# Making gate and up of a ternary feed-forward beside the self-attention, and sharing the program's end between two engines

## The chip, the cores and the metric

The kernel runs on one core of a Trainium2 chip. The metric is the device time of one execution in microseconds, as the median of three runs. The core has five engines that run their own instruction queues: TensorE for matmuls (PE in the profile, with its weight loads shown as PEld), VectorE (DVE), ScalarE (ACT), GpSimd (POOL) and SyncE (SP), which here only issues transfers. Each engine takes its queue in the order in which the program was compiled.

## The reference

A decoder of two layers, batch 4, sequence 512, width 512, float32. There are six phases, each followed by a residual addition and a layer norm over the width:

```python
x = layernorm(x + L0_attn(x))          # phase A: one head of 512, rotary positions
x = layernorm(x + L0_xattn(x, ctx))    # phase B: 8 heads over channels, against a context
x = layernorm(x + L0_ffn(x))           # phase C: ternary weights
x = layernorm(x + L1_attn(x))          # phase D: 16 heads
x = layernorm(x + L1_xattn(x, ctx))    # phase E
x = layernorm(x + L1_ffn(x))           # phase F: fp4 weights, then y / rms(y)
```

Two parts bear on the change. The first feed-forward uses weights of three values, made in the kernel from float32 weights:

```python
def weight_quant(w):
    scale = 1.0 / clip(mean(abs(w)), 1e-5)
    return clip(round(w * scale), -1.0, 1.0) / scale

gate = act_quant(x) @ weight_quant(w_gate).T      # w_gate, w_up: 2048 x 512
up   = act_quant(x) @ weight_quant(w_up).T
out  = act_quant(fwht(silu(gate) * up)) @ weight_quant(w_down).T
```

And the very end of the program is, for the last batch, `y / sqrt(mean(y*y) + 1e-6)`, added to x, and the layer norm of the sum, `(x - m) / sqrt(v + 1e-5)`.

## The kernel before

The work is written as generators. Phases A to F exist for each of the four batches (A0 to A3, B0 and so on). `lanes` keeps two such tasks alive, takes a step of each in turn, and starts the next when a task says so. After every step `step` also advances background generators, each beside a fixed stretch of tasks: C0 beside A1 to A3, the weights of phase C ("C") beside B0 to B2, others later. A class `Pipe` delays a piece of work by a number of steps (`later(n, fn)`, run down by `tick`; `drain` runs it empty, a step at a time).

What comes out is a list of instructions for each engine. A scheduler fixes their order at compile time from costs and due times, and `tc.issue_after(x)` keeps an instruction behind x in its own engine's order. Transfers are nearly all issued by SP, in turn; a transfer whose buffer isn't free, or whose data aren't made yet, holds those behind it. Buffers come from pools: "o" with 69 of 2 KB per partition, "w" with four (for raw weights, `tw`), "t" with 13, "x" with 12, and 8 banks of PSUM.

Phase A, for a batch (`l0_attn`): eight products qk of 12 matmuls each (every float32 product is made of a high and a low part, hence three matmuls for one); ACT adds the bias (L340); DVE and POOL turn by the rotary angles (L349 on DVE, L352 on POOL) and POOL joins the halves (L357), after which ACT and POOL split the result into high and low. The values are made next, then four score products `as`, softmax (L398 on DVE, L400 on ACT), the transposed scores as `ap`, cast by ACT to `aph`, and the products `pv` with the values. POOL also adds a bias to x (L408), DVE adds the product and takes statistics (L425, L211), and the norm's root and four norms follow (L217 to L238). The transposed low part of the next x is made by POOL (L146, tile `xTl`).

Phase B, for a batch, has 16 iterations of one shape: six matmuls of scores `bs` (L526), the maximum on DVE (L474), the exponential on ACT (L476), the sum and reciprocal on DVE (L480), a scaling on POOL (L482), eight transposes (L248), copies of these out of PSUM on DVE or ACT (L489) and four products `bo` (L498).

The ternary weights come in 48 chunks of 128x512, 16 for each of gate, up and down (`wg_t`, `wu_t`, `wd_t`). `l0_ffn_scales` (C0) reads all 48 beside A and sums their absolute values on DVE (L558); for each matrix one matmul with ones (L569) adds over partitions, and L571 and L572 make mean and scale. `l0_ffn_weights` ("C") reads all 48 again beside B. DVE multiplies by the scale and adds a large constant, MAGIC, which rounds (L587), and clips to MAGIC-1 to MAGIC+1 (L588); ACT subtracts MAGIC and writes bf16 (L596), two chunks into one tile `tb` of 2 KB, which stays in SBUF for phase C.

The end (`l1_ffn`, last batch): ACT squares the four accumulators with a running sum (L1214), DVE takes the mean (L1217) and the inverse root by a seed and three Newton steps (`rsqrt`, L166 to L176); then for each of four row tiles the scaled addition (L1220) and the statistics (L211, L212); `finish` makes the second root on DVE and the four norms (L235) and stores (L238).

Of the kernel before, what the change touches and what calls it, by code (L numbers as in the profile page):

```python
# [10 lines left out]
F32 = mybir.dt.float32  # L11
F32R = mybir.dt.float32r
F16 = mybir.dt.float16
BF16 = mybir.dt.bfloat16
# [8 lines left out]
P = 128  # L23
NT = 4
# [44 lines left out]
class Net:  # L69
    def __init__(self, ctx, tc, args):  # L70
# [22 lines left out]
        self.gu_codes = scratch("gu_codes", (22, P, 512))  # L93
        self.xd = [args["x"]] + [scratch(f"x{i}", (B, S, D)) for i in range(1, 6)] + [args["out"]]
# [235 lines left out]
    def l0_attn(self, b):  # L330
# [7 lines left out]
        def evac(ps, w, m):  # L338
            z = zs[w, m] = self.t("z")
            nc.scalar.activation(z, ps, AF.Identity, bias=self.qkb[:, w * NT + m : w * NT + m + 1], scale=1.0 if w else P ** -0.5)  # L340
            if m % 2:
                pipe.later(1, turn, w, zs[w, m - 1], z)
# [200 lines left out]
    def l0_ffn_scales(self):  # L543

        nc = self.nc
        self.had = self.c("had", [P, P], F32R)
        self.had16 = self.load(self.c("had16", [P, P]), self.a["had16"])
        f = self.t("had")
        nc.gpsimd.dma_start(f[:, 0:P], self.a["had"])
        pipe = Pipe()  # L550
        pipe.later(3, nc.vector.tensor_copy, self.had, f[:, 0:P])
        for name in self.TERNARY:
            chunks = self.ternary_chunks(name)
            part = self.c(name + "_abs", [P, len(chunks)])

            def absum(f, n):
                with self.tc.issue_after(self.mark.ins):
                    nc.vector.tensor_reduce(part[:, n : n + 1], f, AX.X, ALU.add, apply_absolute_value=True)  # L558

            for n, (k, c, ap) in enumerate(chunks):  # L560
                pipe.tick()
                pipe.later(1, absum, self.load(self.w("tw"), ap), n)
                yield
            yield from pipe.drain()
            m = self.c(name + "_mean", [P, 4])
            nc.vector.tensor_reduce(m[:, 2:3], part, AX.X, ALU.add)
            yield
            ps = self.pb("tot")
            nc.tensor.matmul(ps[:, 0:1], self.ones, m[:, 2:3], start=True, stop=True)  # L569
            yield  # L570
            nc.vector.tensor_scalar(m[:, 0:1], ps[:, 0:1], 1.0 / (len(chunks) * P * 512), 1e-5, ALU.mult, ALU.max)  # L571
            nc.vector.reciprocal(m[:, 1:2], m[:, 0:1])  # L572
            self.mean[name], self.scale[name] = m[:, 0:1], m[:, 1:2]

    def l0_ffn_weights(self):

        nc = self.nc
        yield from self.bg["C0"]
        pipe = Pipe()
        order = [("wg_t", x) for x in self.ternary_chunks("wg_t")]  # L580
        up = [("wu_t", x) for x in self.ternary_chunks("wu_t")]
        order = [e for c in range(4) for e in order[4 * c : 4 * c + 4] + up[4 * c : 4 * c + 4]]
        order += [("wd_t", x) for x in self.ternary_chunks("wd_t")]
        cur = []

        def quant(name, k, c, f):
            nc.vector.tensor_scalar(f, f, self.scale[name], MAGIC, ALU.mult, ALU.add)  # L587
            nc.vector.tensor_scalar(f, f, MAGIC + 1.0, MAGIC - 1.0, ALU.min, ALU.max)  # L588
            pipe.later(1, put, name, k, c, f)

        def put(name, k, c, f):
            if not cur:
                cur.append(self.o("tb", BF16, 1024))
            o = cur[0][:, 0:512] if len(cur) == 1 else cur[0][:, 512:1024]
            cur.append(o)
            nc.scalar.activation(o, f, AF.Copy, bias=-MAGIC)  # L596
            self.tern[name][k, c] = o
            if len(cur) == 3:
                cur.clear()

        for name, (k, c, ap) in order:
            pipe.tick()
            pipe.later(1, quant, name, k, c, self.load(self.w("tw"), ap))
            yield
        yield from pipe.drain()
# [510 lines left out]
    def l1_ffn(self, b):  # L1116
# [31 lines left out]
        def gate(o):  # L1148
            nc.scalar.activation(o, o, AF.Silu)
            y["gate"] = o  # L1150
# [43 lines left out]
        if b + 1 < B:  # L1194
# [16 lines left out]
            return  # L1211
        for i in range(NT):
            sq = self.t("fsq")
            nc.scalar.activation(sq, acc[i], AF.Square, accum_out=ss[:, i : i + 1])  # L1214
            if i % 2:
                yield
        nc.vector.tensor_scalar(ve, ss, 1.0 / 512.0, 1e-6, ALU.mult, ALU.add)  # L1217
        r = self.rsqrt(ve, fm[:, 8:20])
        for i in range(NT):
            nc.vector.scalar_tensor_tensor(x[i], acc[i], r[:, i : i + 1], x[i], ALU.mult, ALU.add)  # L1220
            self.ln_stats(x[i], i, ln)
            if i % 2:
                yield
        self.finish(pipe, x, ln, 5, b)
        yield from pipe.drain()
# [35 lines left out]
def body(tc, args, phases=range(6)):  # L1261
    with ExitStack() as ctx:
# [4 lines left out]
        net.bg = {("B", 0): net.l0_xattn_ctx(0), "C0": net.l0_ffn_scales(), "C": net.l0_ffn_weights(), "D": net.l1_attn_weights(), "F0": net.l1_ffn_codes(), "F": net.l1_ffn_weights()}  # L1267
# [82 lines left out]
```

## Time and profile before

| | us |
| --- | --- |
| median of three runs | 1586.2 (1585.69 to 1587.84) |
| profiled execution | 1587.75 |
| its span, first to last instruction | 1586.0 |
| mean granted TensorE clock | 0.993 |

In the lists of operations, each line gives the source line, the engine, the operation and the tiles, then shapes and the count; behind the bar come the time in all, the mean of one in ns, and how long the engine sat idle before them with what ended that. Some rows of operations that the change touches or adds to, by source line:

| line | engine | what | count | ns each |
| --- | --- | --- | --- | --- |
| L587 | DVE | scale and round a chunk | 48 | 480 median |
| L588 | DVE | clip a chunk | 48 | 414 median, 384 to 1379 |
| L596 | ACT | chunk to bf16 | 48 | 626 median |
| L340 | ACT | bias to a product of phase A | 32 | 690 median |
| L408 | POOL | bias to x in phase A | 16 | 1306 median, 1289 to 1827 |
| L482 | POOL | scale an exponential in phase B | 128 | 766 mean |
| L1149 | ACT | table load, once, at 1269 us | 1 | 1283 |

In the profile's 40 slices, the busy share of each engine in tenths runs so:

```
PE   8999999999999999899999999999999999999995
DVE  6486589999976688778577697766886897889896
ACT  5333337888878877787696765968635455545552
POOL 6663663555535303430435323353234344434341
```

A slice is 39.65 us. The first six are phase A and the next five or so are phase B. The lists of transfers give a mean time from issue to landing of 3.8 us for the 32 loads of gate chunks, 3.7 for up and 2.8 for down, 256 KB each.

### The profile page before, as it was taken

Reading aid. Unit: us, or ns where it says so; the run is one execution under the profiler, and the core shown is the slowest. Engines: PE = TensorE matmul, PEld = TensorE weight load, DVE = VectorE, ACT = ScalarE, POOL = GpSimd, SP = SyncE. Lnnn points to the kernel's source line nnn. Section 1 sums busy time; section 2 is a strip of 40 time slices with the busy share of each in tenths; the row PEclk is TensorE's granted clock in tenths of the full one; section 3 lists DMA queues with packets and bytes.
Section 4 is the critical chain, followed back from the end, with each engine's and each line's share of the span. In section 5 each row is a group of like instructions: output and inputs, shape, how many; then the busy total and the mean of one; then the engine's idle time right before and its main releaser. Section 6 shows DMA issues by size and latency. Waiting matters only on the chain.

```text
span 1586.0 us, 25593 instructions
## 1 busy us (share of the span) xinstructions
PE 1515.5 (96%) x8222; PEld 1092.0 (69%) x8222; DVE 1239.8 (78%) x2676; ACT 1014.6 (64%) x2193; POOL 666.0 (42%) x672
## 2 busy tenths in 40 slices
PE   8999999999999999899999999999999999999995
PEld 6888785444544664477777768777687767787874
DVE  6486589999976688778577697766886897889896
ACT  5333337888878877787696765968635455545552
POOL 6663663555535303430435323353234344434341
PEclk9999999999999999999999999999999999999998
DMA  7053344455114644653444435543426630020101
GB/s 254 29 166 114 121 155 136 141 173 184 62 57 123 220 150 131 204 178 116 134 109 122 111 131 153 156 112 91 136 99 219 236 107 30 1 80 1 54 1 53
DMA packets 134149, 192.31 MB, mean 121 GB/s; under 512 B 17264, under 2 KB 52080, under 8 KB 134016
## 3 DMA queue, kind: packets, MB, share of 16 engines
q1 hardware_dynamic: 129888, 182.23, 36.3%
q0 software_dynamic: 4128, 8.46, 2.1%
q8 instruction: 65, 1.06, 0.3%
q14 instruction: 68, 0.56, 0.1%
HBM read 117.75 MB, written 47.71 MB: 104 GB/s over the span
## 4 chain that ended last, share of the span: by engine, by line
PE 61%; DVE 17%; ACT 8%; issue 7%; DMA 3%; POOL 3%; SPq 0%; DVEq 0%; ACTq 0%; POOLq 0%
PE fg L1185 7%; PE facc L1168 6%; PE dT L933 3%; DVE fg L1141 3%; DVE bsm L474 3%; PE pg L687 2%; PE pu L689 2%; PE dn L741 2%; ACT de L923 2%; PE had L755 2%; PE bo L498 2%; PE do L953 2%; PE qk L156 2%; PE qk L155 2%; PE qk L154 2%
## 5 line engine op out<-in xcount | busy, mean ns | idle before, releaser
L1141 DVE SCALAR_TENSOR_TENSOR fg<-fg,gs,fg 128x512 f32<-128x512 f32 x220 | 162.7, 744 | 29.1 <-ACT fg L1133 16.0
L923 ACT ACTIVATE de<-de,dm 128x128 f32<-128x128 f32 (+3 forms) x256 | 143.0, 563 | 11.4 <-DVE dm L919 11.0
L1185 PE MATMUL fg<-fxh,gu 128*128 128x512 f32 x352 | 140.4, 399 | 6.0 <-DVE fg L1141 4.3
L919 DVE CUSTOM_DVE_ANT_0 de<-ds,negm,thr 128x128 f32<-128x128 f32 (+3 forms) x256 | 126.3, 545 | 19.0 <-PE ds L908 15.8
L482 POOL TENSOR_SCALAR be<-be,bsm 128x512 f32<-128x512 f32 x128 | 96.4, 766 | 103.8 <-DVE bsm L480 68.2
L1185 PE MATMUL fg<-fxl,gu 128*128 128x512 f32 x352 | 137.3, 390 | 0.0
L664 POOL TENSOR_TENSOR hl<-g,hh 128x512 fp32r<-128x512 f32 x64 | 83.3, 1308 | 110.6 <-ACT hh L663 89.8
L1145 POOL TENSOR_TENSOR fg<-fg,fg 128x512 f32<-128x512 f32 x44 | 60.4, 1374 | 150.0 <-DVE fg L1141 54.7
L476 ACT ACTIVATE be<-bs,bsm 128x512 f32<-128x512 f32 x128 | 87.4, 690 | 31.1 <-DVE bsm L474 29.3
L845 POOL TENSOR_TENSOR dql<-dqf,dqh 128x512 fp32r<-128x512 f32 x32 | 41.4, 1294 | 150.6 <-ACT dqh L844 141.6
L933 PE MATMUL dT<-ident,de 128*128 128x128 f32 x640 | 91.3, 278 | 8.5 <-ACT de L923 6.4
L933 PEld LDWEIGHTS dT<-ident,de 128*128 128x128 f32 x640 | 71.7, 141 | 27.6 <-ACT de L923 14.8
L1185 PEld LDWEIGHTS fg<-fxh,gu 128*128 128x128 f32 x352 | 66.0, 188 | 31.2 <-DVE fg L1141 15.6
L474 DVE TENSOR_REDUCE bsm<-bs 128x1 f32<-128x512 f32 x128 | 83.3, 671 | 0.0
L498 PE MATMUL bo<-bpT,cT 128*64 128x512 f32 x256 | 77.0, 618 | 2.7 <-DVE bpT L489 1.4
L248 PEld LDWEIGHTS bT<-ident,be 128*128 128x128 f32 x512 | 54.9, 141 | 34.1 <-issue 10.4
L248 PE MATMUL bT<-ident,be 128*128 128x128 f32 x512 | 73.2, 281 | 3.7 <-POOL be L482 2.2
L1185 PEld LDWEIGHTS fg<-fxl,gu 128*128 128x128 f32 x352 | 66.1, 188 | 12.2
L352 POOL TENSOR_TENSOR z<-z,rope_cos 128x512 f32<-128x512 f32 x32 | 46.8, 1473 | 64.8 <-DVE zs L349 57.8
L1137 ACT ACTIVATE fg<-fg,gs 128x512 f32<-128x512 f32 x44 | 30.3, 689 | 67.3 <-PE fg L1185 67.2
L687 PE MATMUL pg<-qT,tb 128*128 128x512 bf16 x256 | 66.8, 381 | 4.5 <-ACT qT L649 2.8
L1133 ACT ACTIVATE fg<-fg,gs 128x512 f32<-128x512 f32 x88 | 60.1, 683 | 16.4 <-PE fg L1185 16.3
(342 smaller groups left out, 4673.2 us busy)
## 6 DMA issues: line engine op xcount, KB each, us to landing
x<-x SPq DMA_DIRECT2D x176, 256.0 KB, 3.0
had_scratch<-hw SPq DMA_DIRECT2D x64, 256.0 KB, 2.3
z<-had_scratch SPq DMA_DIRECT2D x64, 256.0 KB, 6.0
stk<-dqh SPq DMA_DIRECT2D x192, 64.0 KB, 2.1
tw<-in_wg_t SPq DMA_DIRECT2D x32, 256.0 KB, 3.8
tw<-in_wu_t SPq DMA_DIRECT2D x32, 256.0 KB, 3.7
tw<-in_wd_t SPq DMA_DIRECT2D x32, 256.0 KB, 2.8
p<-in_gu_p SPq DMA_DIRECT2D x22, 256.0 KB, 3.1
```

The lines of the kernel that those rows point to most:

```text
L248: self.nc.tensor.transpose(pt[:, i * P : (i + 1) * P], srcs[i][:, j * P : (j + 1) * P], self.ident)
L474: nc.vector.tensor_reduce(sm[:, h : h + 1], ps, AX.X, ALU.max, negate=True)
L476: nc.scalar.activation(e, ps, AF.Exp, bias=sm[:, h : h + 1], accum_out=sm[:, 2 + h : 3 + h])
L482: nc.gpsimd.tensor_scalar(es[h][i], es[h][i], sm[:, 4 + h : 5 + h], 1.0, ALU.mult, ALU.mult)
L498: nc.tensor.matmul(po[0][h * 64 : h * 64 + 64, :], cT[j][:, c : c + 64], pTs[h], start=j == 0, stop=j == NT - 1)
L687: nc.tensor.matmul(pg, tern["wg_t"][k, c][:, m], qT[k], start=k == 0, stop=k == NT - 1)
L919: nc.vector.tensor_tensor_reduce(es[i], ps, self.negm[:, 384 - P * i :], -1.0, self.thr[:, i : i + 1], ALU.add, ALU.min, n4[:, i : i + 1])
L923: nc.scalar.activation(es[i], es[i], AF.Exp, bias=n4[:, i : i + 1], scale=-1.0, accum_out=den[:, hh * 4 + i : hh * 4 + i + 1])
L933: nc.tensor.transpose(pt[:, o + (i - j) * P : o + (i - j + 1) * P], es[i][:, j * P : (j + 1) * P], self.ident)
L1141: self.emitted["DVE"] = nc.vector.scalar_tensor_tensor(y[u], ps, s, y[u], ALU.mult, ALU.add)
L1168: nc.tensor.matmul(acc[t], h[l][:, c], self.dn[i][r], start=i == 0 and n == 0, stop=i == 10 and n == 2)
L1185: nc.tensor.matmul(ps, self.gu[i, u][:, g * P : (g + 1) * P], xT[g][n], start=n == 0, stop=n == 1)
```

## The change

The change has two parts that don't meet.

*Ternary weights.* A helper `ternary` gives a function that quantises a chunk, in one of two ways. The old way (for down) leaves the two passes on DVE. The early way (for gate and up) does the multiplication and rounding on ACT, the clip on POOL and the conversion on ACT. `l0_ffn_scales` becomes `l0_ffn_ternary`: while it reads up's chunks for the absolute sum it reads gate's chunks a second time, into tiles `tq` of pool "o", and quantises them in the early way; while it reads down's it does so for up. The result, a `tb` tile of 256 KB for each two chunks, is stored to memory (`tern_kept`, eight tiles for each matrix). The early ACT operations are kept behind the latest L340 operation, and the clips behind the latest join. Between the matrices the pipe isn't drained any more, but ticked. `l0_ffn_weights`, beside B, quantises only down's 16 chunks, and loads the 16 kept tiles.

*The end.* For the last batch an ACT table with Ln and Exp is loaded after the last Silu. Both inverse roots become Ln and Exp(-0.5 x) on ACT with one Newton step on DVE. The statistics of the sum are no longer made by L211 and L212: DVE's addition accumulates the row sum, and ACT squares the tile with a running sum. Two of the four norms go to ACT.

Instructions, before and after: DVE 2665 and 2579, ACT 1761 and 1804, POOL 677 and 709, SP 840 and 872; PE's number stays.

```diff
+    def ternary(self, pipe, name, done, early=False):
+        def quant(n, f):
+            if early:
+                with self.tc.issue_after(self.turned.ins):
+                    nc.scalar.activation(f, f, AF.Copy, bias=MAGIC, scale=self.scale[name])
+                pipe.later(1, clip, n, f)
+            else:
+                nc.vector.tensor_scalar(f, f, self.scale[name], MAGIC, ALU.mult, ALU.add)
+                nc.vector.tensor_scalar(f, f, MAGIC + 1.0, MAGIC - 1.0, ALU.min, ALU.max)
+                pipe.later(1, put, n, f)
+
+        def clip(n, f):
+            with self.tc.issue_after(self.joined.ins):
+                nc.gpsimd.tensor_scalar(f, f, MAGIC + 1.0, MAGIC - 1.0, ALU.min, ALU.max)
+            pipe.later(3, put, n, f)
+
+        def put(n, f):
+            if n % 2 == 0:
+                cur.append(self.o("tb", BF16, 1024))
+            o = cur[0]
+            with self.tc.issue_after(self.turned.ins):
+                nc.scalar.activation(o[:, n % 2 * 512 : n % 2 * 512 + 512], f, AF.Copy, bias=-MAGIC)
+            if n % 2:
+                cur.clear()
+                done(n // 2, o)
...
-    def l0_ffn_scales(self):
+    def l0_ffn_ternary(self):
...
+        def keep(name, n, o):
+            pipe.later(1, lambda: nc.sync.dma_start(self.tern_kept[name][n], o.bitcast(F32)))
+
+        old = None
+        for new in self.TERNARY:
...
+            for n in range(len(chunks)):
                 pipe.tick()
-                pipe.later(1, absum, self.load(self.w("tw"), ap), n)
+                pipe.later(1, absum, self.load(self.w("tw"), chunks[n][2]), part, n)
+                if old:
+                    pipe.later(2, quant, n, self.load(self.o("tq"), todo[n][2]))
                 yield
...
     def l0_ffn_weights(self):
...
+        order = [(name, n) for c in range(0, 8, 2) for name in self.TERNARY[:2] for n in (c, c + 1)]
+        quant = self.ternary(pipe, "wd_t", lambda n, o: use("wd_t", n, o))
+        for n, (name, m) in enumerate(order):
+            pipe.tick()
+            pipe.later(1, quant, n, self.load(self.w("tw"), self.ternary_chunks("wd_t")[n][2]))
+            yield
+            pipe.tick()
+            o = self.o("tb", BF16, 1024)
+            self.load(o.bitcast(F32), self.tern_kept[name][m])
+            use(name, m, o)
+            yield
             yield
...
+        with self.tc.issue_after(self.silu.ins):
+            table = self.tc.keep_in_program_order(nc.scalar.preload_act_table_set(LOG_EXP))
+
+        def root(ve, y, t):
+            with self.tc.issue_after(table.ins):
+                nc.scalar.activation(y, ve, AF.Ln)
+            nc.scalar.activation(y, y, AF.Exp, scale=-0.5)
+            self.newton(ve, y, t)
...
+        root(ve, r, fm[:, 12:16])
+        tot, sqs, mean, m2, v2, r2, t2, off = (ln[:, 4 * n : 4 * n + 4] for n in range(8))
+        for i in range(NT):
+            nc.vector.scalar_tensor_tensor(x[i], acc[i], r[:, i : i + 1], x[i], ALU.mult, ALU.add, accum_out=tot[:, i : i + 1])
+            sq = self.t("fsq")
+            nc.scalar.activation(sq, x[i], AF.Square, accum_out=sqs[:, i : i + 1])
+        nc.vector.tensor_scalar(mean, tot, 1.0 / 512.0, None, ALU.mult)
+        nc.vector.tensor_tensor(m2, mean, mean, ALU.mult)
+        nc.vector.tensor_scalar(m2, m2, 1e-5, None, ALU.subtract)
+        nc.vector.scalar_tensor_tensor(v2, sqs, 1.0 / 512.0, m2, ALU.mult, ALU.subtract)
+        root(v2, r2, t2)
+        nc.vector.scalar_tensor_tensor(off, mean, -1.0, r2, ALU.mult, ALU.mult)
+        for i in range(NT):
             if i % 2:
+                nc.vector.tensor_scalar(x[i], x[i], mean[:, i : i + 1], r2[:, i : i + 1], ALU.subtract, ALU.mult)
+            else:
+                nc.scalar.activation(x[i], x[i], AF.Identity, bias=off[:, i : i + 1], scale=r2[:, i : i + 1])
+            nc.sync.dma_start(self.xd[6][b, i * P : (i + 1) * P, :], x[i])
```

## The prediction

> **What bounds the kernel now.** I read the page's two tables first, then the windows of the two stages that the change touches, then the waits, the chain and the timeline there.
>
> ```profile
> PE 1515.5 (96%) x8222; PEld 1092.0 (69%) x8222; DVE 1239.8 (78%) x2676; ACT 1014.6 (64%) x2193; POOL 666.0 (42%) x672
> ```
>
> TensorE (PE) is busy for 96% of the span, so a gain must come from the remaining 70.5 us in which it isn't, or from places where its work is stretched out. The windows show two different stages: the self-attention A (the first 240 us) and, from about 240 to 446 us, the cross-attention B, beside which the ternary weights are made.
>
> ```profile
> core 0: us, PE busy (x) PEld busy (x) DVE busy (x) ACT busy (x) POOL busy (x), PEclk, DMA share, GB/s
> 120.00:160.00 40.00, 40.00 (x186) 33.07 (x186) 25.69 (x46) 12.83 (x24) 16.67 (x13) 1.00 0.32 103
> 160.00:200.00 40.00, 38.26 (x170) 30.42 (x169) 21.11 (x35) 14.16 (x27) 25.83 (x20) 1.00 0.41 132
> ...
> 267.00:318.00 51.00, 47.93 (x270) 23.71 (x270) 48.73 (x103) 45.03 (x108) 29.44 (x36) 1.00 0.51 159
> 318.00:366.00 48.00, 47.05 (x270) 23.87 (x269) 46.84 (x103) 42.12 (x103) 27.49 (x33) 1.00 0.55 167
> 366.00:413.00 47.00, 44.85 (x259) 22.62 (x258) 46.04 (x105) 40.93 (x102) 27.07 (x34) 1.00 0.40 135
> 413.00:446.00 33.00, 32.74 (x204) 17.11 (x200) 28.59 (x64) 26.26 (x67) 16.70 (x25) 1.00 0.19 65
> ```
>
> In A, PE has no gap and ScalarE (ACT) is one third busy, GpSimd (POOL) one half to two thirds. In B, VectorE (DVE) is the full engine: 48.73 + 46.84 + 46.04 = 141.6 of 146 us, 97%. In the last window, where no ternary work is left, it falls to 28.59 of 33, 87%. The waits between 235 and 446 us agree:
>
> ```profile
> POOL be L482 <- DVE bsm L480: 66.6, 33, 22.3
> ACT be L476 <- DVE bsm L474: 29.3, 39, 3.8
> ```
>
> POOL and ACT both stand waiting for DVE's softmax pieces. How far this stretches PE is seen in the distance between the score matmuls of consecutive iterations (64 in the stage). Undisturbed iterations look like this on PE's timeline:
>
> ```profile
> 300.74 0.49 PE L526 MATMUL bs<-kh,qh 64*128 64x512 f32 x2
> ...
> 303.66 0.51 PE L526 MATMUL bs<-kh,qh 64*128 64x512 f32 x2
> ...
> 306.60 0.50 PE L526 MATMUL bs<-kh,qh 64*128 64x512 f32 x2
> ```
>
> That is 2.92 us an iteration. From 267 to 318 us there are 15 iterations in 51.3 us between first and last score matmul, 7.5 above 15 x 2.92; from 318 to 366, 15 in 48.25, 4.45 above; from 366 to 413, 14 in 46.34, 5.46 above. The sum is 17.4 us. After 413, 11 iterations take 32.49, only 0.37 above. So the excess goes when the ternary work goes.
>
> **The change part by part.**
>
> *1. Less DVE work in B.* The two quantising passes (L587, L588) take 7.08 + 7.86 + 5.55 and 7.50 + 7.26 + 5.37 us in the three windows, 40.6 of DVE's 141.6. Of 48 chunks 32 leave (gate and up), and down's 16 are spread over the same stretch, so about 2/3 x 40.6 = 27 goes: DVE falls to 114.5 of 146, 78%. That is below the 87% at which the last window kept the floor, so most of the 17.4 us should come back. The three longest iterations (4.79, 4.52 and 4.29 us) hold 4.8 of the excess and may belong to the changeover between batches, where a norm and the next queries are made; I leave half of that. **-15 us**. Bounds: -9 (two thirds of 17.4, less half of those 4.8) and -18 (all of it, with part of the 1.9 us of excess in 8 iterations before 267). ACT also loses 32 of the 48 L596 conversions here (0.63 us each, 20 us of its 128), and the queue of SP swaps 32 weight loads for 16 of the kept tiles.
>
> *2. More work in A.* Each of 32 chunks now costs there one more load (issue about 0.45 us on SP; landing 3.7 us by the rows of the same loads), one ACT pass with scale and bias (0.72 us, by L630 of that form), one POOL clip (0.77 us, by L482, the nearest POOL tensor_scalar), one ACT conversion (0.63 us, L596) and half a store. That is 32 x 1.35 = 43 us of ACT over some 160 us in which it is 35% busy, and 25 us of POOL, 60% busy: room on average. What counts is the order, as both engines take their queues strictly in turn, and PE has nothing in reserve. The one PE gap in A shows where:
>
> ```profile
> 161.02 1.29 POOL z L352
> ...
> 165.18 1.74 POOL x L408 x2
> ...
> 168.36 3.00 POOL x L408 x2
> 171.35 4.97 POOL xTl L146 x4
> 176.37 0.50 PE qk L155
> ```
>
> The chain before A3's first product runs through POOL from 161 to 176.3, and PE took 5.6 us for a product that otherwise takes 2.72, a stall of 2.9. In the compiled order of the changed kernel four clips stand between the last joins and the fourth xTl: 4 x 0.72 = 2.9 us more on exactly this chain. **+3** (0 if the additions L408 drift behind, 5 if a clip also waits for its ACT pass), and **+0.5** for the product after it.
>
> [...] The trace has 766 ns for POOL's L482 against a 414 ns median for DVE's clip L588. [...]
>
> *3. The passage from A to B.* Before B0, the order puts 12 more ACT operations between the last exponentials of A3 (ae, at 238.1 and 238.7) and the last aph casts (done at 244.0), which feed the value products pv from 244.1. At a spacing of 0.53 us (as the aph and qh casts at 240.34, 240.82, 241.35 show) they take 6.4 us. In addition some of these chunks' loads stand on SP's queue behind transfers that wait for POOL's additions (about 229 us), for the norm's stores (about 235) and for a kept tile's own store, so ACT waits in turn. Followed by hand with these durations, the last aph comes 4 us late if the loads have landed, 10 us if not, and PE has some 2 us of score products to fill in. **+6** (2 to 11, nearer to neither end).
>
> *4. The end.* Only the last batch is changed. Its timeline today:
>
> ```profile
> 1569.47 0.17 DVE L1217 TENSOR_SCALAR fm<-fm 128x4 f32<-128x4 f32 x1 [7.18 <-ACT fsq L1214]
> 1569.67 0.17 DVE L166 TENSOR_SCALAR fm<-fm 128x4 int32<-128x4 int32 x1
> ...
> 1571.85 1.41 DVE L1220 SCALAR_TENSOR_TENSOR x<-facc,fm,x 128x512 f32<-128x512 f32 x2
> ...
> 1577.97 0.17 DVE L220 TENSOR_SCALAR ln<-ln 128x4 f32<-128x4 f32 x1
> ...
> 1580.35 1.91 DVE L235 TENSOR_SCALAR x<-x,ln 128x512 f32<-128x512 f32 x4
> 1580.93 1.79 SPq L238 DMA_DIRECT2D out_dram<-x  x4
> ```
>
> Each inverse root takes 1571.85 - 1569.67 = 2.18 us in eleven small DVE steps. The new one is Ln and Exp on ACT (0.205 us each, as L223 and L224 show on the same 128x4), one Newton step (3 x 0.2), and a crossing each way of 0.05 or so: about 1.09. Two of them: -2.2. The sums and statistics run from 1571.85 to 1577.97, 6.1 us, on DVE alone. Now DVE does four sums with an accumulator (0.61 us spacing and a 0.08 read, by L1041) and ACT follows with a Square each (0.60 and a 0.20 read, as in fsq), then four small steps: 0.69 + 4 x 0.67 + 4 x 0.2 = about 4.2, -2.0. One more small step for the offset, +0.2. The four norms (1.91) split over two engines gain little, as SP issues the four stores one by one (1.79 for the four): +0.1. **-3.9** (-3 to -4.6). An extra table load on ACT stands after the last Silu. The trace's only such load costs 1.283 us (L1149), and ACT idles 3.82 us before fsq at 1566.77, so it is hidden. Without that cover, up to 1.3 us would come back.
>
> [...]
>
> *5. The rest.* The DMA queues move 192 MB before and some 8 MB more after (32 loads of 256 KB; the kept stores and loads weigh about as much as the 32 reloads they replace), at half load. The feed-forward C finds its weights ready either way, and PE order there is unchanged. 0 (+-1).
>
> Sum: -15 + 3.5 + 6 - 3.9 = -9.4. The profiled execution is 1587.75 (span 1586.0, 1.7 around it); it stands 1.5 above the median 1586.2. From it the sum gives 1578.3, from the median 1576.8. As the result will be a median, I take **1577**.
>
> **The rivals.**
>
> *A hides nearly all.* The early work finds room and only half a microsecond is lost, while all the excess returns: -17.4 - 3.9 + 0.5, **1565**. For it: ACT has two thirds free in A. Against it: the chain through POOL above, which has no slack.
>
> *B isn't released.* ACT (128 of 146 us there, 88%) or POOL's and PE's own sequence holds the pace, and only half of 15 returns: -7.5 + 9.5 - 3.9 = -1.9, **1584**. For it: L474's waits may only move to ACT. Against it: the window after 413, where ACT is at 80% and the floor is held; ACT loses 20 us here too.
>
> *Slower: head-of-line waiting in A.* POOL's clip waits for ACT's pass, that for a load, that for SP's queue, and behind each stand the joins and casts that feed PE at 100%. If every clip, and not four of them, lands on the path to PE, A pays 32 x 0.72 = 23 us, and with the passage's 6 this is 29, against 18.9 gained: +10, **1596**. It decides from 18.9 us of loss in A and its passage. For it: one queue order for all batches. Against it: the joins have 40% of slack on POOL, except at the start of a batch.
>
> *The change doesn't do what it says.* If the kept tiles came back late in B, the feed-forward would wait. They are used first after 446 and are loaded from 225 on, 16 tiles at about 3 us (the page's other 256 KB loads): I give it no share of its own.
>
> **How the numbers follow.** Forecast, 1570 to 1583: 0.50. A hides all: 0.17. B not released: 0.19, of which a quarter is below 1583.0 and three quarters within the bound. Slower: 0.14. What a measurement of this kernel can tell from no change is 0.2%, 3.2 us: faster is below 1583.0, slower above 1589.4. Faster = 0.50 + 0.17 + 0.05 = 0.72; same 0.14; slower 0.14. The low end adds the best bounds, -18 + 0 + 2 - 4.6 = -20.6, which gives 1566 and takes in the first rival; the high end the middle loss at A3, a late passage and the worst of the rest, -9 + 5.5 + 8.5 - 3 = +2, which gives 1588. What is left out is the slower rival and little else. The likeliest case alone: 1570 to 1583.
>
> **What would show it.** Right: B's DVE share near 78% and its iterations near 2.92 us throughout, with L474's wait on ACT shrunk (step 1); a gap before A3's first product of about 6 us instead of 2.9 (step 2); A3's first pv some 12 us after its last ae instead of 6 (step 3); from the last fsq to the end about 12.7 instead of 16.5 us (step 4). It would be wrong if PE shows gaps elsewhere in A (third rival), if the iterations stay above 3.1 us with DVE at 78% (second), or if C begins with a wait for tb.

## The result, and the profile after

The changed kernel is slower: 1594.5 us (median of 6 runs, 1590.3 to 1596.2) against 1586.5 (1585.7 to 1591.3). The ratio is 1.0044, with a 95% interval of 1.0031 to 1.0057. The profiled execution has a span of 1594.5 us against 1586.0.

Where the 8.5 us went can be read place by place, because TensorE does nearly the same matmuls in nearly the same order in both kernels. For each matmul I subtract its start before from its start after. That lag stays flat where nothing changes and steps where time is lost or won. The table gives its steps in the two profiled executions beside the terms of the prediction.

| place | step of the lag, us | predicted |
| --- | --- | --- |
| start of A3, 170 to 176 us | +3.0 | +3 |
| A2's value products, 214 us | +2.0 | +0.5 |
| passage from A to B, 239 to 262 us | +18.6 | +6 (2 to 11) |
| B, 262 to 446 us | -13.5 | -15 (-9 to -18) |
| all later phases | +2.7 | 0 (+-1) |
| behind the last matmul | -4.4 | -3.9 |
| sum (0.1 lies ahead of A3) | +8.5 | -9.4 |

The windows after show the two big terms. Columns as before.

```profile
core 0: us, PE busy (x) PEld busy (x) DVE busy (x) ACT busy (x) POOL busy (x), PEclk, DMA share, GB/s
...
240.00:267.00 27.00, 12.88 (x52) 9.17 (x51) 11.72 (x26) 15.56 (x33) 3.85 (x6) 0.64 0.67 219
267.00:318.00 51.00, 51.00 (x288) 29.49 (x287) 46.11 (x98) 39.50 (x100) 29.62 (x36) 0.99 0.39 124
318.00:366.00 48.00, 47.44 (x286) 24.72 (x284) 41.72 (x91) 40.89 (x102) 28.35 (x35) 1.00 0.49 160
366.00:413.00 47.00, 46.04 (x282) 24.11 (x278) 41.02 (x89) 39.24 (x98) 28.87 (x39) 1.00 0.38 129
```

At the passage PE is busy for 12.9 of 27 us, and so is every other engine only in part: all of them wait for each other. In B the iterations went back to 2.92 us nearly throughout: of the last 54 of the 63 distances between iterations, 30 were under 3.0 us before and 45 are after. DVE's share of the three windows is 46.1 + 41.7 + 41.0 = 128.9 of 146 us, 88%, where I had 78%. But the windows now hold more of B's work. Over the same matmuls, from 267 to 413 us before (first line) and from 290.1 to 423.8 after (second line), DVE's busy time fell by 25.6 us, close to the 27 foreseen; its share is 87% because the stretch itself became 12.3 us shorter:

```profile
267.00:413.00 146.00, 139.83 (x794) 70.19 (x796) 141.61 (x308) 128.07 (x311) 84.00 (x102) 1.00 0.49 154
```

```profile
290.10:423.80 133.70, 131.90 (x796) 68.63 (x794) 116.06 (x247) 114.03 (x283) 82.97 (x105) 1.00 0.42 137
```

The timeline of the passage shows who holds whom: ScalarE's early pass is L554 now, the exponentials are L401, the norm's root L221 to L225 and its four norms L236, its stores L239.

```profile
237.20 0.72 ACT L554 ACTIVATE tq<-tq,wu_t_mean 128x512 f32<-128x512 f32 x1 [7.63 <-DMA tq<-in_wu_t]
...
238.88 0.67 ACT L401 ACTIVATE ae<-as,asm 128x512 f32<-128x512 f32 x1
...
246.36 0.72 ACT L554 ACTIVATE tq<-tq,wu_t_mean 128x512 f32<-128x512 f32 x1 [6.72 <-DMA tq<-in_wu_t]
...
247.70 0.19 ACT L225 ACTIVATE ln<-ln 128x4 f32<-128x4 f32 x1
...
258.97 0.72 ACT L554 ACTIVATE tq<-tq,wu_t_mean 128x512 f32<-128x512 f32 x1 [3.16 <-DMA tq<-in_wu_t]
...
235.68 0.17 DVE L221 TENSOR_SCALAR ln<-ln 128x4 f32<-128x4 f32 x1
...
247.92 0.58 DVE L175 TENSOR_TENSOR ln<-ln 128x4 f32<-128x4 f32 x1 [11.48 <-ACT ln L225]
...
225.59 7.40 SPq L253 DMA_DIRECT2D tq<-in_wu_t  x2
...
240.71 0.86 SPq L253 DMA_DIRECT2D tq<-in_wu_t  x2
...
249.50 0.33 SPq L239 DMA_DIRECT2D x<-x  x1
...
252.41 0.43 SPq L253 DMA_DIRECT2D tq<-in_wu_t  x1
...
248.61 0.48 PE L249 MATMUL ap<-ident,ae 128*128 128x128 f32 x1 [4.04 <-ACT ae L401]
252.31 0.47 PE L249 MATMUL ap<-ident,ae 128*128 128x128 f32 x1 [3.23 <-ACT ae L401]
...
262.88 1.22 PE L527 MATMUL bs<-kh,qh 64*128 64x512 f32 x4 [5.93 <-ACT qh L470]
```

ACT stands 7.6, 6.7 and 3.2 us for loads of `tq`. Behind the second of these loads stand the norm's Ln and Exp (L225 at 247.70), so DVE, which had asked for them at 235.7, idles 11.5 us. Behind the norm on DVE stand the last row maxima, and on SP the norm's stores, which go out at 249.5 only; and behind these stand the next loads of `tq` (252.41), for which ACT waits again until 258.97. That is a loop through three queues: from SP to ACT, to DVE and back to SP. SP's own waits between 200 and 270 us name its links:

```profile
SPq L594 <- ACT tb L571: 14.7, 5, 5.5
SPq L253 <- DVE wd_t_abs L591: 12.3, 6, 7.2
SPq L239 <- DVE x L236: 6.9, 1, 6.9
SPq L253 <- POOL x L409: 6.7, 1, 6.7
```

### The profile page after: what moved, and what is told of

Read it like the earlier page. It is cut to its first block, busy times and chain, and to the rows that moved or that the text cites. A ratio compares the mean times of both kernels' runs of the same rounds, so it can differ in the third digit from the quotient of the medians.

```text
span 1594.5 us, 25701 instructions
## 1 busy us (share of the span) xinstructions
PE 1516.0 (95%) x8222; PEld 1094.8 (69%) x8222; DVE 1211.0 (76%) x2594; ACT 1040.2 (65%) x2240; POOL 686.5 (43%) x704
## 4 chain that ended last, share of the span: by engine, by line
PE 60%; DVE 14%; ACT 11%; issue 6%; DMA 5%; POOL 4%; SPq 0%; ACTq 0%; DVEq 0%; POOLq 0%
PE fg L1226 7%; PE facc L1209 5%; PE dT L974 3%; DVE fg L1182 3%; PE do L994 2%; ACT de L964 2%; PE dn L782 2%; PE bo L499 2%; PE pg L728 2%; PE pv L155 2%; DVE bsm L475 2%; PE pv L157 2%; PE pv L156 2%; PE ds L949 2%; PE pu L730 2%
## 5 line engine op out<-in xcount | busy, mean ns | idle before, releaser
L475 DVE TENSOR_REDUCE bsm<-bs 128x1 f32<-128x512 f32 x128 | 83.0, 675 | 0.1
L1226 PEld LDWEIGHTS fg<-fxl,gu 128*128 128x128 f32 x352 | 66.1, 188 | 12.3
L249 PEld LDWEIGHTS bT<-ident,be 128*128 128x128 f32 x512 | 54.9, 141 | 28.2 <-issue 12.5
L499 PE MATMUL bo<-bpT,cT 128*64 128x512 f32 x256 | 71.4, 618 | 1.0 <-ACT bpT L490 1.0
L1209 PE MATMUL facc<-p4h,fhh 128*128 128x512 f32 x176 | 69.6, 396 | 0.4 <-DVE fg L1182 0.3
```

Of the source, the lines that this page charges most:

```text
L249: self.nc.tensor.transpose(pt[:, i * P : (i + 1) * P], srcs[i][:, j * P : (j + 1) * P], self.ident)
L475: nc.vector.tensor_reduce(sm[:, h : h + 1], ps, AX.X, ALU.max, negate=True)
L499: nc.tensor.matmul(po[0][h * 64 : h * 64 + 64, :], cT[j][:, c : c + 64], pTs[h], start=j == 0, stop=j == NT - 1)
L1209: nc.tensor.matmul(acc[t], h[l][:, c], self.dn[i][r], start=i == 0 and n == 0, stop=i == 10 and n == 2)
L1226: nc.tensor.matmul(ps, self.gu[i, u][:, g * P : (g + 1) * P], xT[g][n], start=n == 0, stop=n == 1)
```

## The experiments

The table gives the lag of matmuls in us, read as above against the kernel before, at four points (235 is ahead of the passage, 255 behind it, 448 behind B, "last" the last matmuls), then the median and the ratio to before. The first microseconds of the program move by up to 1.5 us between executions, in e13 by 2, in unchanged code; a phase near 1200 us moves by 2 or more, also where nothing was changed ahead of it (the run of the end alone). So single figures of lag are good to 1 or 2 us ahead of B and 3 at the last matmuls.

| run | 235 | 255 | 448 | last | median | ratio (95%) |
| --- | --- | --- | --- | --- | --- | --- |
| changed kernel | 5.1 | 23.6 | 10.2 | 12.9 | 1594.5 | 1.0044 (1.0031, 1.0057) |
| e1 end only | 1.1 | 1.2 | 0.2 | 1.7 | 1581.6 | 0.9971 (0.9959, 0.9983) |
| e2 ternary only | 8.0 | 25.7 | 12.1 | 11.9 | 1599.1 | 1.0078 (1.0058, 1.0098) |
| e3 gate only | 3.4 | 2.6 | 0.1 | 4.3 | 1586.7 | 0.9999 (0.9986, 1.0011) |
| e4 no up loads | 7.5 | 13.6 | 0.0 | 3.9 | 1586.9 | 0.9996 (0.9982, 1.0010) |
| e5 start in A0 | 22.8 | 22.1 | 9.9 | 9.8 | 1593.1 | 1.0036 (1.0024, 1.0048) |
| e6 store by ACT | 6.4 | 20.3 | 6.6 | 11.9 | 1592.0 | 1.0024 (1.0014, 1.0034) |
| e7 clip on DVE | 8.3 | 18.7 | 5.1 | 4.0 | 1590.6 | 1.0015 (1.0003, 1.0027) |
| e8 e5 and e7 | 26.4 | 25.6 | 13.3 | 12.6 | 1598.0 | 1.0067 (1.0054, 1.0080) |
| e9 half of up | 8.4 | 15.5 | 5.7 | 3.4 | 1586.3 | 0.9995 (0.9984, 1.0005) |
| e10 gate, spread | 3.0 | 3.5 | 0.3 | -0.9 | 1583.2 | 0.9984 (0.9975, 0.9993) |
| e11 end, spread | 0.2 | 1.4 | 4.2 | 6.0 | 1586.7 | 1.0002 (0.9992, 1.0012) |
| e12 loads ahead | 7.1 | 18.5 | 5.0 | 6.9 | 1588.7 | 1.0016 (1.0004, 1.0027) |
| e13 eight early | 6.1 | 6.4 | 8.3 | 6.4 | 1590.5 | 1.0023 (1.0010, 1.0035) |
| e14 no early work | 1.0 | 0.4 | -11.5 | -12.9 | 1570.0 | 0.9889 (0.9873, 0.9904) |
| e15 e6 and e12 | 7.8 | 18.9 | 5.2 | 5.9 | 1590.7 | 1.0027 (1.0015, 1.0039) |
| e16 clip on POOL in B | 0.6 | 0.4 | 1.3 | 1.4 | 1586.9 | 1.0005 (0.9990, 1.0019) |

### The two parts alone: e1, e2

e1 takes the functions of the end from the changed kernel and the rest from before; e2 the other way.

> The kernel before with the change of the end alone. Theory: the end gains by itself what the changed kernel shows behind its last matmul, 12.9 us of lag at the last matmuls against 8.5 at the span's end, so -4.4 us: about 1582.1, ratio 0.997. Rival: the end's gain depends on the late state of the rest (transfers or DVE work still outstanding), then under 2 us of gain, above 1584.5.

> The changed kernel with the old end. Theory: the ternary part alone carries the whole loss: matmuls late by 3 us at the start of A3, 5 before the passage from A to B, about 23.6 behind it, 10 after B, 13 at the end; time about 1599, ratio 1.008. Rival: the two parts are not additive, the time is within 2 us of 1594.5.

Both came as expected: 1581.6 and 1599.1. The parts add (-5.1 and +12.5 against +8 together). The end alone is faster than both kernels, and of all the runs that compute everything (e4 and e14 do not) it is the fastest.

### What the passage waits for: e4, e6, e12, e15

```diff
e4:
+                src = self.rope_cos if name == "wu_t" else f
...
-                    nc.scalar.activation(f, f, AF.Copy, bias=MAGIC, scale=self.scale[name])
+                    nc.scalar.activation(f, src, AF.Copy, bias=MAGIC, scale=self.scale[name])
...
-                    pipe.later(2, quant, n, self.load(self.o("tq"), todo[n][2]))
+                    f = self.o("tq")
+                    pipe.later(2, quant, n, f if old == "wu_t" else self.load(f, todo[n][2]))
e6:
-            pipe.later(1, lambda: nc.sync.dma_start(...))
+            pipe.later(1, lambda: nc.scalar.dma_start(...))
e12:
+                while old and len(raw) < min(16, n + 5):
+                    raw.append(self.load(self.o("tq"), todo[len(raw)][2]))
...
-                    pipe.later(2, quant, n, self.load(self.o("tq"), todo[n][2]))
+                    pipe.later(2, quant, n, raw[n])
```

> The changed kernel without the second loads of up: ScalarE's early pass for up reads a resident table instead of the loaded chunk, so up's codes are those of that table; every ScalarE and GpSimd operation and every store stays. Theory (ScalarE waits for loads that SP issues late): lag added at the passage falls from 18.6 to 7 or less, the time to 1583 or less. Rival (the 12 added ScalarE operations and the stores make the loss by themselves): 12 us or more of the passage's lag stay, the time is 1588 or more.

> The changed kernel with the kept tiles' stores issued by ScalarE, which makes them, in place of SP. Nothing else differs. If the stores are a link of the loop (SP waited 14.7 us for ScalarE's conversions around the passage), up's loads are issued sooner: the passage's lag falls from 18.6 to 8 to 14 us, time 1584 to 1591. If the loads are late for other reasons (the buffers, the absolute sums, the norm's stores), it stays within 3 us of 18.6, time 1592 or more.

> The changed kernel with the early chunks' loads issued four steps sooner; operations, their order on ScalarE and GpSimd and the number of loads stay. If the loads are late because SP reaches them late, the passage's 18.6 us go to 10 or less, near the 6 us without any loads: 1583 to 1587. If they are late because their buffers come free late, or hold SP in another place, 14 us or more stay: 1590 or more.

> The changed kernel with both of the runs that each eased the passage: up's and gate's loads four steps sooner (7.6 us of the passage's 18.6 gone by itself) and the kept tiles' stores issued by ScalarE (4.7 gone). If each breaks its own link of the loop, they add: the passage keeps 5 to 8 us, what it cost without any loads of up (6.2): 1582 to 1586. If they break the same link, it keeps 10 or more: 1588 or more.

Without up's loads the passage costs 13.6 - 7.5 = 6.1 us in place of 18.6. All of ScalarE's and GpSimd's work is still there (for up, ScalarE reads a table that lies in SBUF already, so what comes out are not up's codes). ACT is busy for 12.5 of the 15 us shown and waits for no load, though the queues move 283 to 347 GB/s here too:

```profile
235.00:240.00 5.00, 5.00 (x24) 4.14 (x23) 4.27 (x12) 3.56 (x10) 1.69 (x3) 1.00 0.87 299
240.00:245.00 5.00, 5.00 (x24) 4.14 (x23) 1.87 (x4) 5.00 (x11) 1.84 (x3) 1.00 0.91 347
245.00:250.00 5.00, 3.78 (x27) 3.17 (x25) 3.21 (x8) 3.95 (x8) 1.32 (x3) 1.00 0.87 283
```

So of 18.6 us about 6 are the early operations that stand among the passage's own, and 12.5 go with late loads. Without these operations the passage adds nothing: in e14, below, the lag is 1.0 us ahead of it and 0.4 behind. The median of e4, 1586.9, stayed above the 1583 that I had named, though the lag went as the theory says; A took 2.4 us more ahead of the passage.

Stores by ACT alone leave 13.9 us (1592.0, just above the range that I had named), loads four steps ahead 11.4, which lies between my two cases. Both together leave 11.1, so the two gains don't add; my expectation of 5 to 8 was wrong. ACT's waits for `tq` between 225 and 272 us are 19.0 us in the changed kernel, 10.4 in e6, 7.9 in e12 and 11.4 in e15. Two other waits are long there, one of ACT (first line, e12, from 225 to 272 us) and one of SP (second line, e15, from 200 to 270 us; 12.3 in the changed kernel):

```profile
ACT tb L571 <- POOL x L409: 8.0, 1, 8.0
```

```profile
SPq L253 <- DVE wd_t_abs L591: 26.4, 13, 6.9
```

So where one link of the loop is eased another holds: GpSimd's additions in e12, the buffers that DVE's absolute sums free in e15. Whether easing these too would free the passage was not tested.

### Moving the early work: e3, e5, e9, e13

e3 makes gate alone early (up on DVE beside B), e9 gate and half of up, e13 gate's first eight chunks; e5 makes all of it, but starts sooner:

```diff
e3:
-            old = new
+            old = new if new == "wg_t" else None
...
e9:
-                if old:
+                if old == "wg_t" or old and n < 8:
...
e13:
-                if old:
+                if old == "wg_t" and n < 8:
...
e5:
-                    if plain.index(first) < n <= plain.index(last) + 1:
+                    if plain.index(first) < n <= plain.index(last) + 1 or key == "C0" and n == 1 and hasattr(net, "joined"):
```

> The changed kernel, but only gate is made ternary early; up is made on DVE beside B, as before. Theory (a loop of waits through four in-order queues at the passage, fed by up's late loads): without up's loads there the passage's 18.6 us of lag go to under 3; A3's start keeps its 3; B gives back about half of 13.5, 7; with the end's 4.4 the time is about 1579 to 1582. Rival (the passage is slow for any added work or for the new order of the absolute sums): at least 9 us of the passage's lag stay and the time is 1586 or more.

> The changed kernel, with its early work started some steps sooner, inside the first self-attention, so that the last early operation of every engine is ordered before the last softmax of the self-attention. All of the work stays. Theory (the loop needs early loads and ScalarE work among the passage's own operations): the passage adds under 2 us of lag instead of 18.6, A's starts keep 3 to 6, B gives back 12 to 14, the end 4.4: 1574 to 1579, ratio 0.993 to 0.995. Rival (the work as such is too much for A, wherever it lies): the lag appears at other places of A, in sum at least 15 us before B, and the time is 1585 or more.

> The changed kernel with gate and the first half of up made early; the second half of up is made on DVE beside B (24 chunks there in 48 steps, against 16 after and 48 before). Theory (the passage is slow because up's last early chunks lie in it): the passage's 18.6 us of lag go to 3 or less; A3's start and the turn at 214 us keep 3 to 5; B gives back about 10; with the end's 4.4: 1579 to 1583. Rival (any early up work loses as much, as the early start did in other places): 10 us or more of lag are added after 180 us and the time is 1588 or more.

> Only gate's first eight chunks are made early, which ends before A3 starts; the other 40 are made on DVE beside B in 48 steps, with the new end. Theory (A's losses come from early work at the start of A3 and at the passage): no lag over 1 us in A, B gives back 2 to 4, the end 4.4: 1578 to 1581, below the end alone (1581.6). Rival (each early chunk costs A, wherever it lies, or 40 chunks saturate B as 48 do): 1581 to 1585.

The passage's loss goes with the early work in it: nothing in e3 and e5, though 7.1 us in e9 (1586.3 us), where I expected 3 at most. But e5 loses as much elsewhere. It has 22.8 us of lag ahead of the passage: 4.0 at 58 us, 5.9 at the value products at 106, 4.9 at A3's start and 8.0 at the value products at 214. That is the rival's reading, and for e5 it decides against mine: the earlier start moved the loss and did not lessen it. The work alone doesn't fix the size, though. Gate's half (e3) costs 2.6 us up to 255 us, both halves 23.6, and with all of the work in place, but a changed order or engine, e6, e7 and e12 have 20.3, 18.7 and 18.5. Eight chunks in e13, all over before A3 starts, cost 4 us there:

```profile
168.08 4.52 DVE L236 TENSOR_SCALAR x<-x,ln 128x512 f32<-128x512 f32 x3
172.52 1.74 DVE L147 TENSOR_TENSOR qkl<-z,qkh 128x512 fp32r<-128x512 f32 x1
...
166.91 5.41 POOL L409 TENSOR_TENSOR x<-x,bvo 128x512 f32<-128x512 f32 x4
```

These are e13's rows of DVE and POOL at A3's start, where the scores `as` wait for `qkl`. Two clips had put a pair of POOL's joins back by 2 to 3 us, and a conversion ahead of the root on ACT (L225 at 161.8, before at 157.4, of which 2 us are this run's lag from its first microseconds) the norm; so the three norms L236 fell beside POOL's additions and took 1.5 us each, where the four at the end of the program before took 1.91 together. So a delay of two or three microseconds became 4. In B e13 loses 1.9 us with its 40 chunks, where I expected 2 to 4 back, and its 1590.5 lies above both of my cases.

e3 gained 2.5 us in B where I expected 7, and its 1586.7 lies in the rival's range, though the rival's lag at the passage is not there. Whether the density of its 32 chunks beside B is the reason is what e10 tests below.

### GpSimd's clips: e7, e8

```diff
-            with self.tc.issue_after(self.joined.ins):
-                nc.gpsimd.tensor_scalar(f, f, MAGIC + 1.0, MAGIC - 1.0, ALU.min, ALU.max)
+            with self.tc.issue_after(self.mark.ins):
+                nc.vector.tensor_scalar(f, f, MAGIC + 1.0, MAGIC - 1.0, ALU.min, ALU.max)
```

> The changed kernel with the early clips on VectorE in place of GpSimd. Theory (four clips in GpSimd's queue before the fourth low part of the next x make A3 start 3 us late): that lag goes to 1 us or less; the passage's 18.6 stays within 4, as its loads are as late as before: 1590 to 1596. Rival (A3 starts late because ScalarE is late with its casts): 2 us or more of the 3 stay.

> Both: the early start inside the first self-attention, and the clips on VectorE. If the two losses are independent, A costs under 3 us in sum, B gives back 12 to 14, the end 4.4: 1570 to 1576, 2 to 5 below the early start alone. If VectorE's place in A is needed for the rotary turns, A loses 4 us or more and it is slower than the early start alone.

With the clips on DVE, GpSimd is early again: its four xTl end at 176.7 us in e7 (176.3 before, 179.6 in the changed kernel), so the clips were what held that chain. But the lag grows by 5.9 us at A3's start (0.7 ahead of it, 6.6 behind) in place of 3.0, as DVE's `qkl` now comes 3.3 and 1.4 us late for the scores. The wait changed its engine. e8 is the slower for it, by 4.9 us against e5.

At the passage e7 missed what I expected: it costs 10.4 us there (8.3 to 18.7), where I had said that it stays within 4 of 18.6, as no load moves. SP's wait for GpSimd's additions (L409, 6.7 us in the list of the changed kernel) is gone from e7's list, and ACT's waits for `tq` are 9.0 us in place of 19.0. So the clips, which stand ahead of the additions, are by this trace a link of the loop too. e4, e6, e7 and e12 each take a part of the same 18.6 us; together they take more than the whole, so none of these parts is the price of one cause alone.

### B by itself: e10, e11, e14, e16

e10 is e3 with its 32 chunks spread over all four batches; e11 is e1 with 48 so spread; e16 is e1 with the clip beside B on GpSimd. e14 is the changed kernel with zeros stored in place of gate and up:

```diff
e14:
-                if old:
-                    pipe.later(2, quant, n, self.load(self.o("tq"), todo[n][2]))
+                if old and n % 2 == 0:
+                    nc.sync.dma_start(self.tern_kept[old][n // 2], self.zero)
...
e10, e11:
-... ("B0", "B2", "C") ...
+... ("B0", "B3", "C") ...
...
e16:
-            nc.vector.tensor_scalar(f, f, MAGIC + 1.0, MAGIC - 1.0, ALU.min, ALU.max)
+            pipe.later(1, clip, name, k, c, f)
...
+            nc.gpsimd.tensor_scalar(f, f, MAGIC + 1.0, MAGIC - 1.0, ALU.min, ALU.max)
```

> Gate alone early, as in the run with only gate, but up's and down's 32 chunks are spread over all four batches of B (one each two steps) in place of 32 in 40 steps. Theory (what costs in B is how densely DVE's passes lie, not their number): B gives back 7 to 10 us in place of 2.5; A3's start keeps 3, the end gains 4.4: 1575 to 1579. Rival (32 chunks cost what they cost): within 2 us of 1586.7.

> The kernel before with the new end, and its 48 chunks beside B spread over all four batches (three in four steps) in place of one a step; nothing early. Theory (density): B gives back 3 to 5 us, A loses nothing, the end gains 4.4: 1576 to 1579. Rival (DVE's sum over B decides, 170 us of its work in 179): within 1.5 us of the end alone, 1581.6.

> The changed kernel without any making of gate and up: no early loads, no early ScalarE or GpSimd operations; the kept tiles are filled with zeros at the same steps, so gate and up are zero; their stores, the loads beside B, down's 16 chunks and the new end stay. It prices B's and the end's gain with the price of A taken out. Theory (gains and losses lie in different places and add): no lag up to the passage, B gives back 13 to 17, the end 4.4: 1566 to 1570. Rival (part of B's gain in the changed kernel is only the passage's lag made good, as queues that waited run ahead): B gives back under 9, 1574 or more.

> The kernel before with the new end, and the clip of its 48 chunks beside B on GpSimd in place of VectorE; nothing moves into A. Theory (B is stretched by VectorE's occupancy, 97% of 146 us): 20 us of VectorE's 141.6 go, and B gives back 3 to 6 us with no loss in A: 1576 to 1579 with the end's 4.4, a version ahead of the end alone. [...]

e14 settles the sum. With A's price taken out B gives back 11.9 us, less than the 13 to 17 that I expected and more than the rival's 9, and the kernel takes 1570.0. So 1.6 of the changed kernel's 13.5 may be lag of the passage made good. The changed kernel takes 24.5 us more than e14: that is the price of making gate and up early, twice what their leaving B is worth. By the lags, 23.2 us of it lie ahead of B (23.6 against 0.4).

The other three correct my picture of B. e10 gave back 3, not 7 to 10 (its 1583.2 lies between my two cases), and e11 lost 3: spreading does not help. e16 is the sharpest. DVE's share over the three windows falls to 43.38 + 42.67 + 41.60 = 127.7 of 146 us, 87%, with nothing gained:

```profile
267.00:318.00 51.00, 47.30 (x272) 23.86 (x270) 43.38 (x89) 44.65 (x109) 38.10 (x50) 1.00 0.51 161
318.00:366.00 48.00, 45.74 (x262) 23.30 (x262) 42.67 (x88) 42.75 (x105) 37.22 (x49) 0.96 0.54 163
366.00:413.00 47.00, 44.94 (x256) 23.02 (x254) 41.60 (x88) 39.08 (x98) 32.78 (x43) 1.00 0.40 131
```

Over the same matmuls as above DVE is busy for 129.0 us in e16 (first line) and 118.1 in e14 (second line), after 141.6 in the kernel before. So e16 takes 12.6 us off DVE, e14 23.5:

```profile
267.30:414.80 147.50, 139.49 (x795) 70.68 (x792) 128.97 (x267) 127.74 (x312) 109.39 (x143) 0.99 0.48 150
```

```profile
266.70:402.00 135.30, 132.61 (x796) 69.00 (x794) 118.08 (x250) 115.56 (x286) 83.55 (x105) 1.00 0.42 141
```

The waits between 267 and 446 us say in part why e16 gains nothing (us in total, times, longest). The first line is of e16, the second of e14; in the kernel before the same wait had 2.2 us.

```profile
PE bT L248 <- POOL be L482: 6.6, 6, 2.1
```

```profile
PE bT L249 <- POOL be L483: 1.6, 4, 0.5
```

PE's transposes wait for GpSimd's scalings, which now stand behind clips. Three distances between iterations are 5.47, 6.38 and 4.56 us, where the longest before was 4.79; of the last 54, 33 are under 3.0 us (30 before, 44 in e14). So less work on DVE is not enough while clips stand in another queue between two steps of a softmax. How much of B's stretch is DVE's own, and how much belongs to ACT's conversions and the loads of gate and up, which e16 leaves in B, was not separated.

## Why the prediction was wrong

**The sign failed on one term.** The passage from A to B (step 3) was set at +6, with 11 as its bound, and measured 18.6. The other 5.3 us between -9.4 and +8.5 are small misses of all the other terms. Behind the 6 stood two parts: ACT's twelve operations, and loads that come late. By the walk the last `aph` came 4 us late for the first part and 6 more for the second, of which PE could fill 2; the runs show 6.1 (e4) and 12.5. For the second I followed each load by hand behind what stood ahead of it, once, and let it land in 3.7 us; in the profile after, the 32 loads took 5.2 in the median and up to 6.5, and the queues moved 306 GB/s between 255 and 260 us. And I stopped at the first round: that the waiting ACT holds the norm's root, the root the norm's stores, and the stores the next loads, so that the lateness returns, was not in the walk. The bound was no bound. The high end of the range took even less for the passage, 8.5; with 11 it would be 1590.7, still below 1594.5.

**The slower rival was right in its mechanism** (head-of-line waiting through SP, ACT and POOL), and its 1596 is near the 1594.5. That nearness is luck in good part: it priced 32 clips on the path to PE at 23 us and the passage at 6, and the runs show 5.1 us of loss in A and 18.6 at the passage. With the clips off GpSimd (e7) the lag behind the passage is still 18.7. e5 shows that starting sooner would not have saved the sum.

**A3's start** came out as its term (+3.0), and e7 confirms the four clips as the cause on GpSimd's side (they took 0.62 to 0.68 us each), but e13 shows a second cause that the step lacks: the norm's root delayed on ACT.

**B** came within its range (-13.5 against -15; -11.9 in e14), and DVE lost nearly what the step said. Its reason, DVE's 97%, was too simple. The 78% divided the work that is left by the old 146 us, though the stretch was to become shorter. ACT's wait for the row maxima (L474, now L475), which was to shrink, is 30.0 us over B after and 29.3 before. And e16 has 12.6 us less on DVE and no gain. I read the share of an engine where the waits of PE, which named POOL and ACT as well, had to be read.

**The end** was sized rightly: -4.4 against -3.9 (e1: -5.1 in the medians). The lines after, with the two roots and the split norms:

```profile
1582.64 0.17 DVE L1266 TENSOR_SCALAR fm<-fm 128x4 f32<-128x4 f32 x1 [7.20 <-ACT fsq L1265]
...
1583.91 0.75 DVE L1272 SCALAR_TENSOR_TENSOR x<-facc,fm,x 128x512 f32<-128x512 f32 x1
...
1587.47 0.16 DVE L1278 SCALAR_TENSOR_TENSOR ln<-ln 128x4 f32<-128x4 f32 x1 [0.18 <-ACT fsq L1274]
...
1588.82 1.00 DVE L1283 TENSOR_SCALAR x<-x,ln 128x512 f32<-128x512 f32 x2
1588.93 1.52 ACT L1285 ACTIVATE x<-x,ln 128x512 f32<-128x512 f32 x2 [0.82 <-DVE ln L1280]
1589.39 1.93 SPq L1286 DMA_DIRECT2D out_dram<-x  x4
```

Each root takes 1.27 us (1582.64 to 1583.91) where it took 2.38, the sums and statistics 3.56 (to 1587.47) where they took 6.12. The table load (1576.1, 1.28 us) ends 2.8 us ahead of the first square at 1580.2, so it is hidden.

**Nothing for the later phases** was off by 2.7 us: 2.2 us come with one wait of the feed-forward for a reloaded chunk at 557 us, 1.6 at 1133, and 1.1 are won back behind. Neither loss is in every run with the ternary part (e2 and e7 lack the first), e16, which makes nothing early, has the first too (+2.1), and the run of the end alone moves as much at 1200, so I take them for the spread of single executions; that was not tested.

## What to carry to other kernels

Idle time of an engine is no room for work as long as its queue is in order and others wait at its points: where TensorE is full and ACT idles two thirds, some 43 us of ACT work (by the prediction's estimate) and 20 of GpSimd's (32 clips of 0.62 us) still cost 24.5 us, though gate's half by itself cost 2.6 ahead of B. Before moving work, follow one full round of waits at the tightest passage, through the queue that issues the transfers too, and ask whether what is held up there holds up the next load; if it does, a hand-walked delay is a lower bound. And price the two halves of a move by separate runs (e14 and the changed kernel): the gain was real and smaller than the price.

## What the runs showed of the hardware

TensorE's granted clock falls in the passage, and stays low while short bursts alternate with gaps (columns as before):

```profile
244.60:247.80 3.20, 0.00 (x0) 0.00 (x0) 0.00 (x0) 1.44 (x5) 0.61 (x1) 1.00 0.77 293
247.80:250.00 2.20, 0.48 (x1) 0.18 (x1) 1.97 (x6) 1.79 (x5) 0.61 (x1) 0.50 0.00 1
...
250.00:255.00 5.00, 1.88 (x8) 1.59 (x9) 2.22 (x5) 3.48 (x8) 0.61 (x1) 0.50 0.92 281
255.00:260.00 5.00, 1.95 (x10) 1.55 (x8) 0.76 (x2) 1.84 (x4) 0.84 (x2) 0.50 0.99 306
...
262.90:268.20 5.30, 5.19 (x17) 3.23 (x18) 5.30 (x11) 5.17 (x11) 0.00 (x0) 0.50 0.31 105
268.30:270.00 1.70, 1.70 (x9) 0.93 (x8) 1.70 (x3) 0.78 (x2) 0.00 (x0) 1.00 0.37 140
```

It is 0.50 from 247.8 us, 3.2 us after PE's last matmul ahead of a gap of 4.0 us, and is back at 1.00 at 268.3, 5.4 us after PE is busy again at 262.9. Until then the pv products start 0.43 us apart, against 0.23 at full clock, so half of these 5.4 us, about 2.7 of the 18.6, are the clock's, by estimate.

VectorE's norms took 1.5 us each beside GpSimd's additions (e13, 168 to 172 us) and 0.48 at the end of the kernel before (1.91 / 4), where GpSimd was still: its last instruction, at 1563.0, took 1.29 us. The additions took 1.35 us each (5.41 / 4). Why the norms take longer beside them no run here shows. The moment at which a batch's norms fall was worth 4 us of VectorE's time: its four took 6.02 us in e13 (4.52 and another 1.50 at 174.2), 1.91 at the program's end.
